# The last pair's exchange through DRAM, and a score product moved in turn 1, in a fused macaron block

## The chip, the cores and the metric

The kernel runs on one core of a Trainium2 chip. The metric is the device time of one execution in microseconds. The profile's time axis starts at the span's start; the span is a little shorter than the device time.

## The reference

The reference is one transformer block of the macaron kind on x of shape 8 x 512 x 128 (batch, tokens, width), all in float32:

```python
x = x + 0.5 * ffn(layernorm(x))
x = x + attn(layernorm(x))
x = x + 0.5 * ffn(layernorm(x))

# attn: 16 heads of rank 64
xq = einsum('btd,hrd->bthr', x, Q); xk = einsum('bud,hrd->buhr', x, K)
a  = softmax(einsum('bthr,buhr->bthu', xq, xk) / sqrt(128), axis=u)
out = einsum('bthu,bud,hde->bte', a, x, VO)

# ffn: three blocks; each: linear, layernorm, gelu, linear, plus its input
# linear: dequantized 128 x 128 weight + bias + low-rank term (rank 32)
```

## The kernel before

**Pairs and turns.** The 16 heads of a batch entry are taken two at a time: a `Pair`, 8 pairs for each of 8 batch entries, 64 in all. Two pairs make a turn, so there are 32 turns (`s` = 0 to 31). Turn 1 handles pairs 2 and 3, turn 31 handles pairs 62 and 63. A turn computes its own pairs' scores and softmax and, at the same time, the sums (softmax times values) of the pairs of the turn before.

**One pair.** For each of four chunks `c` of 128 queries: `scores` makes two products (one for each head) into a PSUM tile `ps`, of which there are two; `maxima` (VectorE) takes the negated row maxima `nm`; `exps` (ScalarE) makes `e` and the row sums; `inverse` and `divide` scale the rows (GpSimd takes one head, ScalarE mostly the other); `turn` (VectorE) transposes `e` in blocks of 32 x 32 into `tr`. What is left of the transposition is an exchange of blocks between the four groups of 32 partitions, done by DMA: `exchange` issues 16 DMAs of 128 KB on SyncE's queue, piece n going from partition group i to group j, from `tr` to `eT`. `attend` then multiplies the values `v` with `eT` into the accumulators `acc`.

**Order.** Everything is laid out with `at(t, function)`. The due times `t` (32 units to a turn) only sort the calls; the instructions are issued in that order, and at the end of the kernel every engine's instructions are chained in it, SyncE's and ScalarE's DMA issues included. So an instruction that waits holds up all that comes after it on its engine. `T_SCORES` and its neighbours in `TIMES` hold the due times of the eight chunks x of a turn (x = 0 to 3 the first pair's, 4 to 7 the second's). In a turn, `a.attend(0, k, 2)`, the first sums, are due at 1.9 + 0.43 k. The second score product (x = 1) is due at 1.05 or 2.0.

**When the exchanges are issued.** The first pair's exchange is due at 16.4, the second's at 27.2; `near` says how many of its 16 pieces go out there. The rest (two, where `near` is `NEAR` = 14) goes out in the next turn at 7.5, between the `send` (7.0) and the `fetch` (8.0) of the feed-forward blocks' own exchange. That exchange (`Exchange`) goes through DRAM: `send` writes `zout` to a DRAM tile `far` with one DMA, `fetch` reads it back into `zin` with four, each of which gathers for one partition group.

**The last pair.** Pair 63 keeps its transposed chunks in two halves of the queries, `trs[0]` (chunks 0 and 1) and `trs[1]` (chunks 2 and 3), 1 MB each. `exchange_halves`, due at 22.9 of turn 31, sends 16 pieces of 64 KB for each half: the first half on SyncE's queue, the second on ScalarE's. `attend_half` multiplies them into the tiles `sum0` and `sum1`, eight products for each half; the second half's products come later on TensorE, between those of the last feed-forward blocks and the last layer norms.

Of the kernel before, what the change touches and what calls it, by code (L numbers as in the profile page):

```python
# [10 lines left out]
F32 = mybir.dt.float32  # L11
# [7 lines left out]
def kernel(  # L19
# [26 lines left out]
    nc = tc.nc  # L46
    B, T, D = x.shape
    H, R, _ = wq.shape
# [5 lines left out]
    P = 128  # L54
    NC = T // P
    Q4 = P // 32
# [9 lines left out]
    dram = ctx.enter_context(  # L66
        tc.tile_pool(name="dram", bufs=2, space=bass.MemoryType.DRAM)
    )
# [18 lines left out]
    def bank(name, tag):  # L87
        if tag == "scores":
            p = psum.tile([P, 2, NC, P], F32, tag=tag, name=name, bufs=2)
            return p[:, 0]  # L90
        return psum.tile([P, NC, P], F32, tag=tag, name=name, bufs=1)
# [51 lines left out]
    def load_projections(g0, g1):  # L143
# [24 lines left out]
        out=bias_bc,  # L168
        in_=biases.rearrange("(k two) d -> two k d", two=2)[0].partition_broadcast(P),
# [8 lines left out]
    def at(t, fn, *args):  # L178
        tasks.append((t, len(tasks), fn, args))
# [298 lines left out]
    NEAR, IDLE = 14, (3.75, 8.9)  # L478
# [5 lines left out]
    class Block:  # L484
# [42 lines left out]
        def second(self):  # L527
            self.po = bank(f"po{self.name}", self.tag)
            nc.tensor.matmul(  # L529
                self.po, lhsT=wT[:, 2 * self.k + 1, :], rhs=self.aT, start=True, stop=True  # L530
            )
# [39 lines left out]
    class Part:  # L571
# [14 lines left out]
        p = property(lambda self: self.banks[self.c][1])  # L586
# [113 lines left out]
    TURNS = B * HP // 2  # L700
# [95 lines left out]
    class Pair:  # L796
# [157 lines left out]

        def exchange_halves(self):

            self.eTs = []
            for h in range(2):
                self.eTs.append(self.half(("eT", "tr")[h], f"eT{h}_").rearrange(
                    "p (i a q) -> p i a q", i=Q4, a=2 * NC  # L960
                ))
                for n in range(Q4 * Q4):
                    i = n % Q4
                    j = (i + n // Q4) % Q4
                    queue = nc.scalar if h else nc.sync
                    queue.dma_start(  # L966
                        out=self.eTs[h][32 * j : 32 * (j + 1), i, :, :].rearrange(
                            "p a q -> p (a q)"
                        ),
                        in_=self.trs[h][32 * i : 32 * (i + 1), j, :, :, :].rearrange(  # L970
                            "p a c r -> p (a c r)"
                        ),
                    )

        def attend_half(self, h, p, j, k):

            nc.tensor.matmul(  # L977
                p, lhsT=self.v[:, k, j, :], rhs=self.eTs[h][:, :, j * NC + k, :],
                start=j == 0 and k == 0, stop=j == 1 and k == NC - 1,
            )  # L980
# [46 lines left out]
    def attn_add(b, a):  # L1027
        oT = work.tile([P, NC, P], F32, tag="oT", name=f"oT{b}", bufs=1)
        nc.vector.tensor_tensor(
            oT.rearrange("p c (i q) -> p i c q", q=32), by_chunks(accs[b][0]), by_chunks(a[0]),  # L1030
            ALU.add,
        )

        def turn():
            po.append(transposed(oT, f"pot{b}", "acc1"))

        def add():
            nc.vector.tensor_tensor(xs[b], xs[b], po[0], ALU.add)

        po = []  # L1040
        return turn, add
# [17 lines left out]
    def lay_turn(s):  # L1059

        t = s * SUP
        two = pairs[2 * s : 2 * s + 2]
        last = s == TURNS - 1
        for x in range(2 * NC):
            m, c = two[x // NC], x % NC

            early = last and x > NC + 1
            T_SCORES, T_MAX, T_EXP, T_INV, T_POOL, T_ACT, T_TURN = TIMES[s > 0]

            at(t + (T_SCORES[x] if x != 1 or not s or s % 4 == 2 else 2.0), m.scores, c)  # L1070
            at(t + (T_MAX[x] if x != NC or not last else 12.59), m.maxima, c)
            at(t + (T_EXP[x] if not early else 17.9 + 1.4 * (c - 2)), m.exps, c)
            at(t + (T_INV[x] if not early else 20.1 + 0.1 * (c - 2)), m.inverse, c)
            at(t + (T_POOL[x] if not early else 20.2 + 1.2 * (c - 2)), m.divide, c, 0, "pool")

            late = s and x > 2 * NC - 3 and not last
            kind = s % 4 if s < TURNS - 6 else 4
            ta = T_ACT[x] if not late else (20.7, (23.7, 23.7, 20.72, 21.1, 23.7)[kind])[x % 2]
            engine = "act" if s or x != 2 * NC - 1 else "pool"
            if late and x % 2 and kind == 3:  # L1080
                engine = "vector"
            at(t + (ta if not early else 20.3 + 0.05 * (c - 2)), m.divide, c, 1, engine)
            u = 21.5 + 1.3 * (c - 2) if early else T_TURN[x] if not late else (21.0, (26.5, 26.5, 22.0, 21.2, 27.15)[kind])[x % 2]
            if last and x in (2, 3):
                u = 11.4 + 1.15 * (x - 2)
            at(t + u, m.turn, c)
        at(t + (12.58 if last else 16.4 if s else 13.8), two[0].exchange)
        if last:
            at(t + 22.9, two[1].exchange_halves)
        else:  # L1090
            near = NEAR if s % 4 != 1 and s else Q4 * Q4
            at(t + (27.2 if s else 24.5), two[1].exchange, 0, near)
            if near < Q4 * Q4:
                at(t + SUP + 7.5, two[1].exchange, near)
        if not last:
            a, b = pairs[2 * s + 2], pairs[2 * s + 3]
            for m, u, d in ((a, 21.9, 23.6), (b, 27.0, 28.7)) if s else ():
                at(t + u, m.project_both)
                at(t + d, m.keep_both)
            if not s:  # L1100
                a.lay_project(0, "acc0", 12.6, 15.15)
                a.lay_project(1, "acc1", 15.0, 15.42)
                at(t + 15.06, b.project_both)
                at(t + 18.0, b.keep_both)
        if s:
            at(t + (23.6 if not last else 19.6), two[0].values)
            at(t + (25.3 if not last else 20.4), two[0].keep_values)
        u, d = (20.2, 22.0) if last else (29.7, 31.4)
        if s:
            at(t + u, two[1].values)  # L1110
            at(t + d, two[1].keep_values)
        else:
            two[1].lay_half_values(0, "acc0", 15.05, 18.1)
            two[1].lay_half_values(1, "acc1", 15.75, 18.2)


        if s:
            a, b = pairs[2 * s - 2], pairs[2 * s - 1]
            for m, j, u in ((a, 0, 1.9), (a, 1, 7.1), (b, 0, 12.2)):
                for k in range(NC):  # L1120
                    at(t + u + 0.43 * k, m.attend, j, k, 2)
            for k in range(2) if last else ():

                at(t + T_SCORES[2 * NC - 2] - 0.02 + 0.005 * k, b.attend, 1, k, 2)
            for k in range(2 if last else 0, NC):
                u = 31.8 if k == NC - 1 and s % 4 == 1 and s > 1 and not last else 18.5 + 0.43 * k
                at(t + u, b.attend, 1, k, 1)
        if s and s % (HP // 2) == 0:
            r = s // (HP // 2) - 1
            done, a = [], []  # L1130
            at(t + 17.85, attn_copy, r, a)
            at(t + 20.7, lambda: done.extend(attn_add(r, a)))
            at(t + 22.5, lambda: done[0]())
            at(t + 22.55, lambda: done[1]())
# [59 lines left out]
    t = {k: T0 + v for k, v in START.items() if isinstance(v, float)}  # L1194
# [40 lines left out]
    for m in lay_parts(0, 0, 1, T0, START, banks, (  # L1235
# [6 lines left out]
        c = m.c  # L1242
# [34 lines left out]
    for s in range(TURNS):  # L1277
        lay_turn(s)


    m = Unit(0, 1)
# [6 lines left out]
    for b in range(B):  # L1288
# [3 lines left out]
        if b > 1:  # L1292
            s = (b - 1) * Q - 2
            t = s * SUP
            m = Unit(0, b, s)
# [5 lines left out]
        if b < B - 1:  # L1301
            s = (b + 1) * Q + 1
            t = s * SUP
            m = Unit(1, b, s)
# [9 lines left out]
    t = TURNS * SUP  # L1314
    a, b = pairs[-2:]
# [62 lines left out]
    for m in lay_parts(1, B - 1, 0, E, END, end_banks, (  # L1378
# [5 lines left out]
        c = m.c  # L1384
        for k in range(NB + 1):
            at(E + END["bias"][c], m.bias, k)
        y = work.tile([P, D], F32, tag="ph", name=f"end{c}", bufs=8)
        queue = nc.scalar if c % 2 else nc.sync
# [3 lines left out]
            out=out[B - 1].rearrange("(p c) d -> p c d", c=NC)[:, c, :], in_=y  # L1392
# [55 lines left out]
```

## Time and profile before

| | us |
|---|---|
| device time, median of 3 runs | 1038.91 (1037.84 to 1040.05) |
| profiled execution: device time | 1039.99 |
| profiled execution: span | 1038.2 |
| TensorE matmul busy in the span | 1023.9 (99%) |
| VectorE busy | 852.6 (82%) |
| ScalarE busy | 783.0 (75%) |
| GpSimd busy | 659.2 (63%) |

TensorE's granted clock is full in all 40 slices of the span. A line of the profile names the line of the kernel (L892 the score products, L1012 the sums, L977 the last pair's sums, L991 the exchanges, L966 the last pair's exchange, L443 and L448 the send and the fetch), the engine (PE TensorE, PEld its weight loads, DVE VectorE, ACT ScalarE, POOL GpSimd, SP SyncE; a q behind the name is the engine's queue, as it issues DMAs), the operation, and out<-in by the program's names. In the timeline the first two numbers are start and duration in us, x is a count, and square brackets hold the idle time before the group and what ended it. In the chain of waits the pieces follow each other back from the last instruction, each one released by the one before.

### The profile page before, as it was taken

What the parts mean: (1) busy time and instruction counts of PE and PEld (TensorE: products, weight loads), DVE (VectorE), ACT (ScalarE), POOL (GpSimd) and SP (SyncE); (2) the same over time, 40 slices, a digit from 0 to 9 for tenths busy, and PEclk for the clock granted to TensorE, in tenths of its full rate; (3) what the DMA queues carried; (4) which work ended last, traced back from release to release, by engine and by line L of the source; (5) the groups of instructions that cost most, each with busy time, mean ns of one, the idle gap of its engine ahead of it and who ended that gap; (6) DMA issues with size and microseconds to landing.
All of it is one profiled execution on the core that took longest, in us unless ns stands there. A gap on an engine that the chain in (4) does not pass through costs nothing.

```text
span 1038.2 us, 15565 instructions
## 1 busy us (share of the span) xinstructions
PE 1023.9 (99%) x4358; PEld 544.2 (52%) x4358; DVE 852.6 (82%) x1606; ACT 783.0 (75%) x1689; POOL 659.2 (63%) x622
## 2 busy tenths in 40 slices
PE   9899999999999999999999999999999999999998
PEld 7465554545555545555544555544555554455556
DVE  6878878888888988888898888888888888877755
ACT  4877778777777877787877877887778887777743
POOL 4667556678567775777567784767857565465523
PEclk9999999999999999999999999999999999999999
DMA  6077765778767886878767887678787777677770
GB/s 194 4 180 184 181 145 142 173 191 203 188 157 183 199 193 168 211 172 205 187 155 189 200 214 173 162 191 205 186 200 179 174 183 172 155 177 180 183 162 21
DMA packets 80892, 179.61 MB, mean 173 GB/s; under 512 B 21212, under 2 KB 41256, under 8 KB 80808
## 3 DMA queue, kind: packets, MB, share of 16 engines
q1 hardware_dynamic: 78440, 177.18, 71.5%
q10 hardware_dynamic: 2368, 1.45, 0.6%
q8 instruction: 36, 0.59, 0.3%
q14 instruction: 48, 0.39, 0.1%
HBM read 23.62 MB, written 20.71 MB: 43 GB/s over the span
## 4 chain that ended last, share of the span: by engine, by line
PE 92%; SPq 3%; DVE 2%; ACT 2%; DMA 1%; issue 1%; POOL 0%; DVEq 0%; ACTq 0%; POOLq 0%
PE acc L1012 40%; PE ps L892 21%; PE pv L852 10%; PE pqk L829 10%; PE po L529 3%; PE py L494 3%; SPq L991 2%; PE py L621 1%; ACT e L904 1%; SPq L966 1%; DVE tr L934 1%; DVE nm L899 1%; PE sum L977 1%; DMA eT<-tr 1%; PE pp L610 0%
## 5 line engine op out<-in xcount | busy, mean ns | idle before, releaser
L916 POOL TENSOR_SCALAR e<-e,rden 128x512 f32<-128x512 f32 x257 | 398.9, 1563 | 227.6 <-DVE rden L911 227.0
L904 ACT ACTIVATE e<-ps,nm 128x512 f32<-128x512 f32 x512 | 345.2, 685 | 169.9 <-DVE nm L899 165.8
L1012 PE MATMUL acc<-eT,v 64*128 64x512 f32 (+1 forms) x1756 | 465.0, 592 | 1.4 <-DMA eT<-tr 0.9
L899 DVE TENSOR_REDUCE nm<-ps 128x2 f32<-128x1024 f32 x256 | 301.6, 1209 | 60.2 <-PE ps L892 59.6
L1012 PEld LDWEIGHTS acc<-eT,v 64*128 64x128 f32 (+1 forms) x1756 | 198.5, 187 | 239.0 <-issue 230.5
L934 DVE STREAM_TRANSPOSE tr<-e 128x1024 f32<-128x1024 f32 x252 | 307.6, 1230 | 16.1 <-POOL e L916 5.3
L892 PE MATMUL ps<-qk 64*128 64x512 f32 x1024 | 252.5, 597 | 1.6 <-ACT e L904 0.9
L920 ACT ACTIVATE e<-e,rden 128x512 f32<-128x512 f32 x249 | 170.0, 725 | 0.6 <-DVE rden L911 0.2
L892 PEld LDWEIGHTS ps<-qk 64*128 64x128 f32 x1024 | 98.7, 186 | 118.0 <-issue 83.7
L852 PE MATMUL pv<-vo_sb,axT 128*128 128x256 f32 x512 | 121.7, 380 | 0.9 <-ACT e L904 0.9
L852 PEld LDWEIGHTS pv<-vo_sb,axT 128*128 128x128 f32 x512 | 94.8, 190 | 29.4 <-issue 12.6
L904 ACT ACTIVATION_READ_ACCUMULATOR e<-ps,nm 128x1 f32 x512 | 103.1, 201 | 0.0
L386 POOL TENSOR_TENSOR rstd<-mv,mhalf 128x4 f32<-128x4 f32 x42 | 43.3, 1030 | 81.1 <-DVE mv L380 80.9
L865 ACT COPY v<-pv 128x512 f32<-128x512 f32 x124 | 66.2, 586 | 32.9 <-PE pv L852 32.8
L399 POOL TENSOR_SCALAR z<-y,rstd 128x128 f32<-128x128 f32 x136 | 79.7, 603 | 3.4
L911 DVE RECIPROCAL rden<-den 128x2 f32<-128x2 f32 x256 | 36.7, 143 | 37.9 <-ACT e L904 36.9
L829 PE MATMUL pqk<-axT,qT_w 128*128 128x512 f32 x122 | 62.4, 593 | 0.0
L829 PE MATMUL pqk<-axT,kT_w 128*128 128x512 f32 x122 | 62.3, 592 | 0.0
L835 ACT COPY qk<-pqk 128x1024 f32<-128x1024 f32 x61 | 60.6, 994 | 2.1 <-PE pqk L829 2.1
L494 PEld LDWEIGHTS py<-wC,hT 128*128 128x128 f32 x336 | 43.2, 192 | 18.8 <-issue 15.4
L535 DVE SCALAR_TENSOR_TENSOR hT<-po,cols,hT 128x512 f32<-128x512 f32 x42 | 31.0, 741 | 22.3 <-PE po L529 21.9
L501 DVE TENSOR_TENSOR y<-py,bias_bc 128x512 f32<-128x512 f32 x42 | 28.5, 678 | 22.5 <-PE py L494 22.3
(162 smaller groups left out, 788.8 us busy)
## 6 DMA issues: line engine op xcount, KB each, us to landing
eT<-tr SPq DMA_DIRECT2D x1008, 128.0 KB, 2.3
far<-zout SPq DMA_DIRECT2D x15, 768.0 KB, 3.7
zin<-far SPq DMA_DIRECT2D x60, 192.0 KB, 3.9
far<-zout SPq DMA_DIRECT2D x10, 512.0 KB, 3.1
zin<-far SPq DMA_DIRECT2D x40, 128.0 KB, 2.9
x<-in_L_attn_x_dram SPq DMA_DIRECT2D x7, 256.0 KB, 5.2
out_dram<-x SPq DMA_DIRECT2D x7, 256.0 KB, 4.1
far<-zout SPq DMA_DIRECT2D x6, 256.0 KB, 2.6
```

The lines of the kernel that those rows point to most:

```text
L399: engine.tensor_scalar(z[:, c, :], self.src[:, c, :], self.rstd[:, c : c + 1], None, ALU.mult)
L494: nc.tensor.matmul(self.py[:, c, :], lhsT=hTs[self.b][:, c, :], rhs=wC[:, self.k, :], start=True, stop=True,)
L829: nc.tensor.matmul(self.pg[:, i, :], lhsT=(qT_w, kT_w)[i][:, self.g, :], rhs=xTs[self.b], start=True, stop=True,)
L852: nc.tensor.matmul(p, lhsT=xTs[self.b][:, c, :], rhs=vo_sb[:, 2 * self.g : 2 * self.g + 2, :], start=True, stop=True,)
L865: nc.scalar.copy(self.v[:, c : c + NC // 2], self.pv[:, c : c + NC // 2])
L892: nc.tensor.matmul(ps[:, j, :], lhsT=self.qk[rows, 0, ts(c, P)], rhs=self.qk[rows, 1, :], start=True, stop=True,)
L899: nc.vector.tensor_reduce(self.nm[:, c, :], self.ps[c], AX.X, ALU.max, negate=True)
L904: nc.scalar.activation(e[:, j, :], self.ps[c][:, j, :], AF.Exp, bias=self.nm[:, c, j : j + 1], accum_out=self.den[:, c, j : j + 1],)
L916: (nc.gpsimd if engine == "pool" else nc.vector).tensor_scalar(e, e, r, None, ALU.mult)
L920: nc.scalar.activation(e, e, AF.Copy, scale=r)
L934: nc.vector.transpose(self.tr[:, :, :, c, :], self.e[c].rearrange("p h (k j r) -> p j (h k) r", j=Q4, r=32),)
L1012: nc.tensor.matmul(accs[self.b][i], lhsT=self.v[rows, k, j, :], rhs=self.eT[rows, :, j * NC + k, :], start=first, stop=end and (j == 1 or ...
```

## The change

1. In turn 1 the second score product (x = 1) gets its due time from the table, 1.05, instead of 2.0; it now comes before the first sums in TensorE's order.
2. In turn 30 `near` is 16 instead of 14: the two pieces of pair 61 that went out in turn 31 between `send` and `fetch` go out with the other fourteen.
3. `exchange_halves` sends the first half by one DMA to a DRAM tile and fetches it back by four. Of the second half's 16 pieces, 4 are issued by SyncE between the write and the fetches, 8 by ScalarE, and 4 by SyncE after the fetches.

```diff
         def exchange_halves(self):
-            self.eTs = []
-            for h in range(2):
-                self.eTs.append(self.half(("eT", "tr")[h], f"eT{h}_").rearrange(
+            self.eTs = [
+                self.half(("eT", "tr")[h], f"eT{h}_").rearrange(
                     "p (i a q) -> p i a q", i=Q4, a=2 * NC
-                ))
-                for n in range(Q4 * Q4):
+                ) for h in range(2)
+            ]
+            far = dram.tile([P, Q4, 4 * NC * 32], F32, tag="half", name="far_half", bufs=1)
+            nc.sync.dma_start(out=far, in_=self.trs[0].rearrange("p j a c r -> p j (a c r)"))
+
+            def second(n0, n1, queue):
+                for n in range(n0, n1):
                     i = n % Q4
                     j = (i + n // Q4) % Q4
-                    queue = nc.scalar if h else nc.sync
                     queue.dma_start(
-                        out=self.eTs[h][32 * j : 32 * (j + 1), i, :, :].rearrange(
+                        out=self.eTs[1][32 * j : 32 * (j + 1), i, :, :].rearrange(
                             "p a q -> p (a q)"
                         ),
-                        in_=self.trs[h][32 * i : 32 * (i + 1), j, :, :, :].rearrange(
+                        in_=self.trs[1][32 * i : 32 * (i + 1), j, :, :, :].rearrange(
                             "p a c r -> p (a c r)"
                         ),
                     )
+
+            second(0, 4, nc.sync)
+            for j in range(Q4):
+                nc.sync.dma_start(
+                    out=self.eTs[0][32 * j : 32 * (j + 1)].rearrange("p i a q -> p i (a q)"),
+                    in_=far.rearrange("(i r) j f -> j r i f", r=32)[j],
+                )
+            second(4, 12, nc.scalar)
+            second(12, 16, nc.sync)
...
-            at(t + (T_SCORES[x] if x != 1 or not s or s % 4 == 2 else 2.0), m.scores, c)
+            at(t + (T_SCORES[x] if x != 1 or s < 2 or s % 4 == 2 else 2.0), m.scores, c)
...
-            near = NEAR if s % 4 != 1 and s else Q4 * Q4
+            near = NEAR if s % 4 != 1 and 0 < s < TURNS - 2 else Q4 * Q4
```

## The prediction

> **What bounds the kernel now.** I read the page first (its chain that ended last and its list of DMA issues), then the chain in order of time at the two places that the change touches (turn 1, turn 31), then the timeline there, the waits, and the DMA answer for short windows.
>
> From the page: the chain's shares by engine, and five rows of DMA issues (KB each, median us from issue to landing).
>
> ```profile
> PE 92%; SPq 3%; DVE 2%; ACT 2%; DMA 1%; issue 1%; POOL 0%; DVEq 0%; ACTq 0%; POOLq 0%
> ...
> eT<-tr SPq DMA_DIRECT2D x1008, 128.0 KB, 2.3
> far<-zout SPq DMA_DIRECT2D x15, 768.0 KB, 3.7
> zin<-far SPq DMA_DIRECT2D x60, 192.0 KB, 3.9
> far<-zout SPq DMA_DIRECT2D x10, 512.0 KB, 3.1
> ...
> far<-zout SPq DMA_DIRECT2D x6, 256.0 KB, 2.6
> ```
>
> TensorE sets the time. The 3% of SPq is some 20 us in two stretches in which TensorE's next product needs the last of 16 issues on SyncE: pair 0's exchange (turn 1) and the last pair's first half (turn 31). Turn 1, TensorE's timeline:
>
> ```profile
> 59.73 1.13 PE L892 MATMUL ps<-qk 64*128 64x512 f32 x4
> 61.75 1.29 PE L1012 MATMUL acc<-eT,v 64*128 64x512 f32 x3 [0.89 <-DMA eT<-tr]
> 62.68 0.59 PE L892 MATMUL ps<-qk 64*128 64x512 f32 x1
> ```
>
> The first score product is done, the sums stand next and wait for pair 0's transfers; the second score product is queued behind the first of the sums. Turn 31, the chain:
>
> ```profile
> 985.29 0.27 issue
> 985.56 5.65 PE acc L1012 x24
> ...
> 1007.56 2.03 DMA eT<-tr
> 1009.59 0.14 issue
> 1009.73 2.40 PE sum L977 x10
> ```
>
> and the timeline (queues and TensorE):
>
> ```profile
> 997.81 10.35 SPq L966 DMA_DIRECT2D eT<-tr  x16
> ...
> 1001.44 8.99 ACTq L966 DMA_DIRECT2D eT<-tr  x14
> ...
> 1006.37 1.88 PE L1012 MATMUL acc<-eT,v 128*128 128x512 f32 x4
> ...
> 1009.73 0.45 PE L977 MATMUL sum<-eT,v 128*128 128x256 f32 x1 [1.48 <-DMA eT<-tr]
> ```
>
> SyncE needs 0.64 us for each issue, 16 of them 10.35 us, and the last one's 64 KB lands 2.03 us after its issue began. TensorE runs out of work at 1008.25 and waits 1.48 us. The second half (ScalarE's queue) lands at about 1012; its first product comes at 1014.03, so it sets nothing.
>
> **Part 1: second score product of turn 1 before the sums.** Its due time goes from 2.0 to 1.05, past the sum due at 1.9. It needs a free score bank (the far projection weights leave theirs when ScalarE's copy ends at 58.89) and qk, so it can run from 60.6 to 61.5, inside the gap. It is 4 passes of 0.215 us = 0.86 us. The sums still start at 61.75 (the last transfer but one lands at 61.66) and their second row half at 62.35 (last one: 59.98 + 2.31 = 62.29), so all that follows on TensorE comes 0.86 us sooner. Can the rest keep up? VectorE takes the second maximum straight after the first (62.83 for 64.36); ScalarE's exponentials of the first two products end at 64.4 and 65.8, and the banks of products 3 and 4 are wanted at 65.8 and 66.6; pair 1's last issue starts at 70.16, lands at 72.5, and is wanted at 73.77 - 0.86 = 72.91. Nothing new is late: 0.86 us, and everything after hangs on TensorE's chain, so it is kept. Bounds: 0 (something in turn 1 takes it back) to 0.9.
>
> **Part 2: turn 30 sends all 16 pieces of pair 61 together.** Two pieces came in turn 31, behind the exchange's send, issued at 980.31. The DMA answer for 980.8 to 981.5 has them:
>
> ```profile
> eT<-tr SPq DMA_DIRECT2D x2, 128.0 KB, 4.7
> ```
>
> 4.7 us instead of 2.3: they land at about 985.0 and 985.7, and TensorE, ready at 985.29, starts at 985.56 and has 24 passes done at 991.22, not at 985.29 + 24 x 0.2145 = 990.44: 0.78 us lost. Moved ahead of the send they land near 982.6. The send and the fetch behind it go back by the two issues, 1.2 us; the fetch ended at 984.82, the next exchange starts at 987.28 (it waits 2.4 us for VectorE), and ScalarE reads zin only at 1000.19, so SyncE's slack covers it; without that slack it would be 1.2 us. Of the 0.78 us, 0.70 passes to the seventh maximum, exponential and value product (994.93 -> 994.23), but pair 62's products, now starting at 999.37, cannot start before its last transfer (996.73 + 2.3 + 0.1 = 999.13). So 0.25 us reaches TensorE's end of work before the last pair: 1008.25 -> 1008.0.
>
> **Part 3: first half through DRAM.** 16 issues of 64 KB become one write of 1 MB and four fetches of 256 KB, with four pieces of the second half between. Step by step:
> - The write needs the first half's transposes (997.5, or 996.8 with part 2) and SyncE (pair 62's issues end at 997.32): issue at 997.4. The three send rows rise by 0.55 us for each 256 KB, so 1 MB lands after 4.25 us: 1001.7.
> - The four pieces wait for the last transpose (1000.14, or 999.4): 4 x 0.64 us on SyncE, until 1002.0, or 1002.7 without part 2's shift. The fetches are queued behind that wait; the write's landing is hidden under it.
> - Four fetch issues took 1.73 to 2.66 us elsewhere: the last starts at about 1003.6. The 192 KB row takes 3.9 us; 256 KB adds 0.14: I take 4.1, landing at 1007.7. In the records each transfer holds one of eight semaphores and waits for the one eight before it, which can put the last fetch behind a piece on ScalarE's queue: +0.4 us, so 1008.1.
>
> Is the transfer itself that quick? The 512 KB send at 99.57, seen from 101 to 108, moved at the first rates below (slices of 0.175 us); the half exchanges on both queues together at the second (last column of the windows view):
>
> ```profile
> GB/s 468 445 398 468 398 351 0 0 0 0 0 0 0 0 29 158 240 281 205 181 334 258 293 299 158 258 234 164 0 0 0 0 0 0 0 0 0 0 0 0
> ...
> 1001.60:1007.50 5.90, 5.90 (x21) 3.17 (x20) 1.65 (x3) 0.36 (x1) 0.00 (x0) 1.00 0.86 203
> ```
>
> A send runs at about 400 GB/s, twice the direct exchange. [...]
>
> TensorE starts the last pair at about 1008.15 instead of 1009.73: 1.58 us, part 2's 0.25 included. The bounds: landing at 1006.8 if the fetch takes 3.2 us (the 128 KB fetches took 2.9), then TensorE's 1008.0 is the limit and the gain 1.73; or, with no shift from part 2, the last issue at 1004.6 and 4.7 us (the longest landing of any far or zin transfer), 1009.3: gain 0.3. What follows moves with TensorE: z, wanted at 1013.7, is ready at 1010.31; the accumulators' sum is ready at 1009.05 for 1011.96.
>
> **Part 4: second half on two queues.** ScalarE's queue issues 8 pieces instead of 16, SyncE 4 before the fetches and 4 after. The last four start at about 1004.2 to 1006.8 and land by 1009 (1011 if they wait for the fetches); wanted at 1014.03 - 1.6 = 1012.4. Cost and gain nothing; the cover is 1.4 us. ScalarE is idle 12.4 us there, so its shorter queue frees no one. [...]
>
> **Sum.** 0.86 + 1.58 = 2.44 us. The profiled execution took 1039.99 us (span 1038.2 and 1.8 around it) and would take 1037.5; it lies 1.1 above the median of the three runs, so the median 1038.91 becomes 1036.5.
>
> **Rivals.**
> - *The fetch is late, or one part is taken back.* The last fetch lands at 1008.7 to 1010, as behind a held semaphore or in contention with ScalarE's pieces; or turn 1's gain is eaten by a later turn. For it: 192 KB fetches at 3.9 us are slow beside 2.9 for 128 KB. Against: TensorE's 92%. Gain 0.9 to 1.9: 1037.0 to 1038.0.
> - *Slower: the detour is bound by bytes.* The half crosses the 16 engines twice. If both legs run at the 203 GB/s of the direct pieces and interleave with them, 2.1 MB + 12 x 64 KB = 2.9 MB take 14.2 us from 999.0: landing at 1013.2, TensorE at 1013.3, +3.6, less 0.86: 1041.6. It decides from a landing at 1010.5 on. Against it: the send's 400 GB/s; for it, the fetch's 158 to 334 GB/s in the same row.
> - *The change does nothing measurable.* Part 1's second product finds its bank or the weight load late and the half lands as before at 1009.6: 1038.9.
>
> **How the numbers follow.** Forecast 0.55 (1036.5; own range 1035.4 to 1037.1, since the three runs differ by 1.1 each way about their median); late fetch or one part lost 0.25 (1037.5); bound by bytes 0.12 (1041.6); nothing 0.08 (1038.9). 0.2% is 2.1 us, about what a measurement of this kernel can tell from no change: faster means below 1036.8. Of the forecast's 0.55 about four fifths lie below that, and of the late case a fifth, with part of a luckier run: 0.52 faster, 0.33 same, 0.15 slower. The range runs from 1035.2 (full 2.6 and a run at the low end) to 1039.4, which leaves the byte-bound case out.
>
> **What would show it.** Right: in turn 1 eight score passes before the sums and no wait of 0.89; pair 61's sums starting without a gap; the first `sum` product within 0.3 us of the last `acc` product; the write landing after 4.2 us and the fetches after 4. Wrong: TensorE waiting over 1 us for the fetch, SyncE's fetches starting after 1004, or a new wait of TensorE in turns 2 to 4 that gives the 0.86 us back.

## The result, and the profile after

| | us |
|---|---|
| before, median of 14 runs | 1038.74 (1037.02 to 1041.22) |
| changed kernel, median of 14 runs | 1041.09 (1038.66 to 1045.11) |
| ratio, 95% interval | 1.0024, 1.0013 to 1.0035 |
| changed kernel, profiled execution | 1042.77, span 1041.0 |

The change makes the kernel slower, by 0.13 to 0.35%. The forecast was 1036.5.

Turn 1 went as forecast. TensorE's timeline of the changed kernel (start, duration, engine, line, operation, count; the sums' line is now L1024; a pass is one matmul instruction, and x counts them):

```profile
59.83 1.99 PE L892 MATMUL ps<-qk 64*128 64x512 f32 x8
61.84 3.86 PE L1024 MATMUL acc<-eT,v 64*128 64x512 f32 x15
```

Eight score passes stand in one row and the wait of 0.89 before the sums is gone.

Turn 31 did not. TensorE's timeline there (L1024 the sums of pair 62, L989 those of the last pair):

```profile
984.37 5.32 PE L1024 MATMUL acc<-eT,v 64*128 64x512 f32 x24
...
999.21 2.81 PE L1024 MATMUL acc<-eT,v 128*128 128x512 f32 x6 [1.22 <-issue]
...
1006.18 1.88 PE L1024 MATMUL acc<-eT,v 128*128 128x512 f32 x4
1010.85 4.01 PE L989 MATMUL sum<-eT,v 128*128 128x256 f32 x10 [2.78 <-DMA eT<-tr]
```

Three things are to be seen: a wait of 1.22 us before pair 62's products that before did not have (kernels without the new exchange have it too, as the last experiment takes up); 2.78 us instead of 1.48 before the last pair's sums; and ten passes that take 4.01 us, where the same ten took 2.40. (The bracket names a piece of the second half, which landed at about the same time. The products read only what the four fetches wrote; the last fetch's last semaphore event is at 1010.61.)

The chain of waits of the changed kernel shows the same end:

```profile
1007.30 3.50 DMA eT<-tr
1010.81 0.04 issue
1010.85 4.01 PE sum L989 x10
```

SyncE's queue in the timeline (L963 the write to DRAM, L969 pieces of the second half, L980 the fetches):

```profile
986.52 10.02 SPq L1003 DMA_DIRECT2D eT<-tr  x16
996.65 0.53 SPq L963 DMA_DIRECT2D far_half<-tr  x1
999.09 3.19 SPq L969 DMA_DIRECT2D eT<-tr  x4
1002.40 2.21 SPq L980 DMA_DIRECT2D eT<-far_half  x4
1004.66 3.94 SPq L969 DMA_DIRECT2D eT<-tr  x4
```

The DMA answers for 996 to 999 and for 1002.3 to 1004.65 (KB each, median us from issue to landing, over those transfers whose landing the view can tell, here two of the four fetches), and the windows view (busy time of PE, PEld, DVE, ACT, POOL; then the granted clock, the DMA share and GB/s):

```profile
far_half<-tr SPq DMA_DIRECT2D x1, 1024.0 KB, 4.7
...
eT<-far_half SPq DMA_DIRECT2D x4, 256.0 KB, 5.3
```

```profile
1003.00:1010.70 7.70, 5.06 (x18) 2.41 (x16) 3.81 (x12) 0.00 (x0) 1.03 (x1) 1.00 0.87 211
1010.70:1014.20 3.50, 3.35 (x8) 2.76 (x9) 0.00 (x0) 0.00 (x0) 0.00 (x0) 0.51 0.00 0
1014.20:1018.00 3.80, 3.80 (x22) 3.01 (x21) 0.69 (x1) 0.93 (x3) 0.00 (x0) 1.00 0.02 4
```

While the fetches are under way the DMA engines are 87% busy and move 211 GB/s. Just as the sums start, the granted clock is 0.51: that is why ten passes take 4.01 us. The page's 40 slices don't show it, since 3.4 us at half speed take 7% off a slice of 26 us and the digit stays 9. The trace's clock record has the half clock from 1010.72 for 3.413 us.

One table serves all kernels below. It is made from the starts of TensorE's products in the profiled executions: from the first score product of turn 1 to that of turn 2; from the first score product of turn 31 to the last pass of pair 62's sums; from there to the last pair's first product; from that to the start of the last instruction. The start-up varies between 28.6 and 30.9 us from one execution to the next, and turns 2 to 30 between 881.2 and 883.5, with no relation to the edits that one execution of each can show, so these pieces tell more than single times.

| kernel | turn 1 | turn 31 to last of pair 62 | wait with it | last pair to end |
|---|---|---|---|---|
| before | 31.39 | 34.66 | 2.07 | 28.42 |
| changed | 30.52 | 35.23 | 3.37 | 30.07 |
| parts 1 and 2, old exchange | 30.52 | 35.57 | 1.20 | 28.38 |
| new exchange alone | 31.37 | 35.12 | 4.17 | 31.27 |
| changed, TensorE filled | 30.52 | 35.69 | 3.33 | 28.45 |
| two queues, alternating | 30.54 | 43.21 | 0.43 | 28.18 |
| fetch alone | 30.52 | 35.59 | 1.24 | 28.47 |
| shared queues, no DRAM | 30.51 | 35.64 | 0.43 | 28.20 |
| part 1 alone | 30.52 | 35.53 | 1.16 | 28.43 |
| part 2 alone | 31.37 | 35.24 | 1.22 | 28.33 |
| 32 whole rows a fetch | 30.51 | 35.67 | 0.95 | 28.45 |
| 128 rows a fetch | 30.52 | 35.49 | 0.43 | 28.38 |
| shared, starting later | 30.53 | 35.46 | 0.43 | 28.19 |

0.43 in the fourth column means no wait: two passes of pair 62 lie between. From before to changed: -0.87 in turn 1, +0.57 and +1.30 up to the last pair, +1.65 behind it, and +0.10 of start-up: +2.75, of the 2.78 between the two profiled executions.

### The profile page after: what moved, and what is told of

It reads as the page before. It is cut to its first block, busy times and chain, and to the rows that moved or that the text cites. A ratio compares the mean times of both kernels' runs of the same rounds, so it can differ in the third digit from the quotient of the medians.

```text
span 1041.0 us, 15560 instructions
## 1 busy us (share of the span) xinstructions
PE 1025.9 (99%) x4358; PEld 550.1 (53%) x4358; DVE 852.6 (82%) x1606; ACT 783.3 (75%) x1689; POOL 660.1 (63%) x622
## 4 chain that ended last, share of the span: by engine, by line
PE 92%; DVE 3%; ACT 2%; DMA 1%; SPq 1%; issue 1%; ACTq 0%; POOL 0%; DVEq 0%; POOLq 0%
PE acc L1024 40%; PE ps L892 20%; PE pv L852 10%; PE pqk L829 10%; PE py L494 3%; PE po L529 3%; PE py L621 2%; DMA eT<-tr 1%; ACT e L904 1%; DVE tr L934 1%; SPq L1003 1%; PE sum L989 1%; DVE nm L899 1%; PE pp L610 0%; PE py L198 0%
## 5 line engine op out<-in xcount | busy, mean ns | idle before, releaser
L1024 PE MATMUL acc<-eT,v 64*128 64x512 f32 (+1 forms) x1756 | 464.9, 592 | 1.2 <-issue 1.2
L1024 PEld LDWEIGHTS acc<-eT,v 64*128 64x128 f32 (+1 forms) x1756 | 201.3, 187 | 235.7 <-issue 229.6
L501 DVE TENSOR_TENSOR y<-py,bias_bc 128x512 f32<-128x512 f32 x42 | 28.5, 678 | 22.5 <-PE py L494 22.3
```

The costliest lines, as they stand in the source:

```text
L1024: nc.tensor.matmul(accs[self.b][i], lhsT=self.v[rows, k, j, :], rhs=self.eT[rows, :, j * NC + k, :], start=first, stop=end and (j == 1 or ...
```

## The experiments

### Parts 1 and 2 with the old exchange

The changed kernel with the old `exchange_halves`.

```diff
-    (the new exchange_halves)
+    (exchange_halves as before: 16 pieces on SyncE, 16 on ScalarE)
```

> The changed kernel with the old exchange of the last pair: the product of turn 1 and the two pieces of turn 30 alone. Theory (the loss is all in the detour through DRAM): the chain reaches the last pair's exchange about 0.8 us sooner, 16 direct issues from 996.7 end with a landing near 1008.4, the last pair's sums start near 1008.5 (1009.73 before), at full clock; about 1037.5 us, 1.2 below before. Rival (the moved pieces of turn 30 or the moved product cost something later): no gain or a loss, 1038.7 or more, and the last pair's sums not before 1009.7.

Measured: 1037.12 (1036.49 to 1038.72, 11 runs) against 1038.52; ratio 0.9986, 0.9978 to 0.9995. TensorE's timeline of this kernel (L977 the last pair's sums):

```profile
1004.35 1.88 PE L1012 MATMUL acc<-eT,v 128*128 128x512 f32 x4
1006.85 2.40 PE L977 MATMUL sum<-eT,v 128*128 128x256 f32 x10 [0.61 <-DMA eT<-tr]
```

The ten passes take 2.40 again. So the loss lies in the new exchange, and the other two parts keep a gain.

### The new exchange alone

Before with only the new `exchange_halves`.

```diff
-    (exchange_halves as before)
+    (the new exchange_halves)
```

> The kernel before with the new exchange of the last pair alone (detour through DRAM, second half on two queues). Theory: the last fetch lands over 6 us after its issue, near 1011.4, TensorE waits over 3 us, its granted clock falls to a half for some 3.4 us and the first ten passes of the last pair's sums take 4.0 us instead of 2.4; about 1042, 3.3 above before. Rival (the detour is harmless, the other two parts brought the loss): about 1038, sums starting by 1009.

Measured: 1043.43 (1040.80 to 1045.20, 6 runs); ratio 1.0042, 1.0027 to 1.0057. Its timeline and windows view:

```profile
1011.59 4.61 PE L989 MATMUL sum<-eT,v 128*128 128x256 f32 x10 [3.58 <-DMA eT<-tr]
```

```profile
1010.50:1017.30 6.80, 5.71 (x16) 4.65 (x17) 0.21 (x1) 0.00 (x0) 0.00 (x0) 0.50 0.07 17
```

A longer wait, 3.58 us, and half the clock for 6.8 us. The exchange alone costs more than the whole change, and it costs twice: in the wait, and behind it.

### TensorE kept busy through the wait

20 transposes of the identity into a PSUM bank that the second half overwrites later, ahead of the last pair's sums; all else as in the changed kernel.

```diff
+    def fill(n):
+        for _ in range(n):
+            nc.tensor.transpose(end_sums[1][:, 0:P], ident, ident)
+
+    at(t + 19.9, fill, 20)
     for i in range(2 * NC):
```

> The changed kernel with 20 transposes of the identity on TensorE (some 2.1 us, into a tile not yet in use) ahead of the last pair's sums, where it waits. Theory (the wait of 2.8 us is what makes the clock fall): the wait is filled, the clock stays at full speed, the first ten passes take 2.4 us instead of 4.0 and the kernel takes 1.6 us less than the changed one: about 1039.5. Rival (the clock falls for another reason, or falls later anyway): no difference from the changed kernel, 1041.

Measured: 1040.15 (1038.96 to 1042.85, 11 runs); ratio 1.0015, 1.0005 to 1.0024. TensorE's timeline:

```profile
1004.05 1.88 PE L1024 MATMUL acc<-eT,v 128*128 128x512 f32 x4
1005.77 2.35 PE L1338 MATMUL sum<-ident 128*128 128x128 f32 x20
1008.67 2.40 PE L989 MATMUL sum<-eT,v 128*128 128x256 f32 x10 [0.55 <-DMA eT<-tr]
```

The sums start no sooner (3.33 in the table, 3.37 without the filling), but the ten passes are back at 2.40 and what follows takes 28.45 instead of 30.07. So 1.6 us of the profiled execution's loss is the clock, which doesn't fall when the wait is filled: its mean is 0.999 or 1.000 in all 11 runs. In the medians it is less, 0.9 us, and the two intervals overlap: of the 14 runs of the changed kernel 9 have a mean granted clock of 0.998, like the profiled one (median 1041.14), and 5 have 1.0 (median 1040.3).

### The direct exchange on two queues, alternating

Parts 1 and 2, and each half's pieces sent in turn by SyncE and ScalarE.

```diff
-    queue = nc.scalar if h else nc.sync
+    queue = nc.scalar if n % 2 else nc.sync
```

> The changed kernel, but both halves of the last pair go directly, without DRAM, each half's 16 pieces alternating between SyncE's and ScalarE's queues. Theory (issue time on one queue was the limit before): 8 issues on each queue from about 997.5, the first half lands near 1005, TensorE goes from its last sums into the last pair's without a wait; about 1036.2. Rival (the 16 DMA engines are the limit, a second queue adds nothing): the first half lands as with one queue, near 1008.4, and the time is that of the kernel with the two small parts alone, 1037.5.

Measured: 1043.76 (1043.15 to 1045.59, 5 runs); ratio 1.0048, 1.0035 to 1.0062: a miss. TensorE's and SyncE's timelines:

```profile
1002.53 5.36 PE L1012 MATMUL acc<-eT,v 128*128 128x512 f32 x6 [6.65 <-DMA eT<-tr]
...
1013.77 2.32 PE L977 MATMUL sum<-eT,v 128*128 128x256 f32 x10
```

```profile
984.98 15.01 SPq L991 DMA_DIRECT2D eT<-tr  x15
1000.16 10.39 SPq L966 DMA_DIRECT2D eT<-tr  x16
```

The last pair's half is in time, but pair 62's exchange (L991) is not: its last two issues come at 998.19 and 999.48 instead of 993 to 994. In the traces of before and of the changed kernel the transfers of both queues share eight semaphores in rotation, and an issue whose semaphore is still held comes when the transfer that holds it has landed (in the changed kernel SyncE's fourth piece of the second half at 1001.78, that landing at 1001.76). ScalarE's first pieces stand ahead of pair 62's last two in that rotation, though pair 62's have the earlier due time. They are issued from 996.14 on and had taken the semaphores that SyncE's last two needed: those two start at 998.19 and 999.48, and the pieces that held theirs landed at 998.17 and 999.46. TensorE waits 6.65 us, and its next six passes take 5.36 us where they took 2.81; the granted clock is 0.74 on average from 1003 to 1012.

### The fetch alone

The changed kernel without the second half's transfers; the second half's products read the first half's tile instead.

```diff
-            second(0, 4, nc.sync)
...
-            second(4, 12, nc.scalar)
-            second(12, 16, nc.sync)
...
-                p, lhsT=self.v[:, k, j, :], rhs=self.eTs[h][:, :, j * NC + k, :],
+                p, lhsT=self.v[:, k, j, :], rhs=self.eTs[0][:, :, j * NC + k, :],
```

> The changed kernel without the transfers of the last pair's second half: its products read the first half's tile again, so the second half's sums are left out. Theory (the fetch was late because the second half's pieces shared the 16 engines with it): the four fetches land about 0.7 us apart instead of 1.4, the last one under 5 us after its issue instead of 6.6, near 1008.5; TensorE waits under 0.7 us and its clock stays full. Rival (the fetch from DRAM is that slow by itself): they land 1.4 us apart, the last 6 us or more after its issue, and TensorE waits 2.5 us or more.

Measured, one execution: 1039.06 (before beside it 1038.53). From the semaphore events, the four fetches:

| | issued | landed | from issue |
|---|---|---|---|
| changed | 1002.40, 1003.21, 1003.56, 1004.05 | 1006.43, 1007.84, 1009.23, 1010.61 | 4.03, 4.63, 5.66, 6.55 |
| fetch alone | 1001.46, 1001.82, 1002.30, 1002.76 | 1004.92, 1006.20, 1007.42, 1008.63 | 3.46, 4.37, 5.13, 5.86 |

With nothing else on the DMA engines the last fetch still takes 5.86 us, and they land 1.24 us apart: 256 KB at about 212 GB/s. The landing is 1.98 us sooner than in the changed kernel; 1.29 of that is the earlier issue (0.31 of it because this execution starts turn 31 sooner), only 0.69 the company of other transfers. Neither expectation is met in full: the gaps and the last landing are nearer to the rival's, but TensorE waits only 0.65 us. The fetch is slow by itself, and not the whole of the delay.

### What is slow in the fetch: rows and partitions

Both as in the fetch alone, and in both the blocks land in other places than the exchange needs. One reads 32 whole rows of 8 KB into their 32 partitions, so its packets are larger (from 999 to 1005, the write's end included, 54 of 182 are under 8 KB, in the fetch alone 312 of 377) but its destination is the same 32 partitions; the other reads one 2 KB block of every row into all 128 partitions, so its packets are small (251 of 348 under 8 KB).

```diff
-    out=self.eTs[0][32 * j : 32 * (j + 1)].rearrange("p i a q -> p i (a q)"),
-    in_=far.rearrange("(i r) j f -> j r i f", r=32)[j],
+    out=self.eTs[0][rows].rearrange("p i a q -> p (i a q)"),       # 32 rows
+    in_=far.rearrange("p j f -> p (j f)")[rows],
```

```diff
+    out=self.eTs[0][:, j, :, :].rearrange("p a q -> p (a q)"),     # 128 rows
+    in_=far[:, j, :],
```

> As the run with the fetch alone (second half's transfers left out), but each of the four fetches reads 32 whole rows of 8 KB back into its 32 partitions, so that blocks are not exchanged. Theory (a fetch into only 32 partitions is slow, whatever it reads): the fetches still land 1.2 us apart, the last 5.5 to 6 us after its issue. Rival (gathering 2 KB pieces at 8 KB distance from DRAM is slow): 0.7 us apart, the last under 4.8 us after its issue.

> As the run with the fetch alone (second half's transfers left out), but each of the four fetches reads one 2 KB piece of every row into all 128 partitions, so that blocks are not exchanged; the pieces in DRAM are 2 KB at 8 KB distance as in the real fetch. Theory (32 partitions are slow): the fetches land 0.7 us apart, the last under 4.8 us after its issue. Rival (the 2 KB pieces are slow): 1.2 us apart, the last 5.5 us or more after its issue.

The DMA answers, 32 whole rows first, 128 rows second (three of the four landings told):

```profile
eT<-far_half SPq DMA_DIRECT2D x4, 256.0 KB, 4.9
```

```profile
eT<-far_half SPq DMA_DIRECT2D x4, 256.0 KB, 3.8
```

Whole rows change little: landings 1004.10, 1005.32, 1006.48, 1007.60, still 1.17 us apart on average. All 128 partitions do: 1005.45, 1006.13, 1007.00, 1007.62, 0.72 us apart, the last 3.98 us after its issue, and TensorE doesn't wait. The 128-row form reads the same bytes of DRAM as the fetch alone, fetch by fetch; only their destination differs. So in these three runs neither the size of the reads nor DRAM sets the price of the fetch, but that each transfer goes into only 32 partitions (1.24 and 1.17 us apart, against 0.72 into 128). The detour as it is cut here, one fetch for each destination group, has to do that. An exchange that sorts the blocks on the way into DRAM, so that each fetch could land in all 128 partitions, was not run; whether the detour has a cheaper form is open.

### Part 1 alone

```diff
-  at(t + (T_SCORES[x] if x != 1 or not s or s % 4 == 2 else 2.0), m.scores, c)
+  at(t + (T_SCORES[x] if x != 1 or s < 2 or s % 4 == 2 else 2.0), m.scores, c)
```

> The kernel before with the turn-1 product alone. Theory: from turn 1's first score product to turn 2's the time falls by 0.87 us (31.39 to 30.52) and nothing after it changes, with pair 62's last transfer landing 2.4 us after its issue and the wait before the last pair's sums at 1.5 us as before; about 1037.8. Rival (the shift is taken back at pair 62's transfers, as it seemed in the changed kernel): the distance from turn 31's first score product to the last sums of pair 62 grows by 0.5 us or more over 34.66.

Measured: 1037.55 (1036.52 to 1039.81, 12 runs) against 1038.53; ratio 0.9990, 0.9980 to 0.9999. Turn 1 takes 30.52, and from turn 31 to the last pair's sums it takes 36.69 (before 36.73), so nothing is given back there. The rival's sign did come, 35.53 up to pair 62's last sums where before took 34.66, since pair 62's last transfer took 3.23 us; but the wait behind it is shorter by as much (1.16 for 2.07). Its sums of pair 61:

```profile
983.86 5.32 PE L1012 MATMUL acc<-eT,v 64*128 64x512 f32 x24
```

24 passes in 5.32 without a wait, though here the two late pieces are where they were before and take 4.1 and 3.9 us.

### Part 2 alone

```diff
-            near = NEAR if s % 4 != 1 and s else Q4 * Q4
+            near = NEAR if s % 4 != 1 and 0 < s < TURNS - 2 else Q4 * Q4
```

> The kernel before with the two moved pieces of turn 30 alone. Theory (the sooner start of the last pair's exchange runs into pair 62's last transfers): pair 61's sums start without their 0.3 us wait, but pair 62's last transfer lands about 3 us after its issue instead of 2.4, its first product waits, and the last pair's sums start where they did (36.7 us after turn 31's first score product): no difference, 1038.6. Rival (the 0.25 us that I forecast are kept): the last pair's sums start 0.2 us sooner, 36.5.

Measured: 1038.42 (1037.40 to 1041.69, 12 runs); ratio 0.9998, 0.9988 to 1.0007. By the times part 2 can't be told from nothing, and 0.25 us can't be excluded either: the interval runs from 1.2 us faster to 0.7 slower. The one profiled execution shows what the rival named: the last pair's sums start 36.46 us after turn 31's first score product, 0.27 sooner than before, although pair 62's last transfer took 2.97 us and its products waited 1.24, as the theory had it. With part 1 beside it the gain isn't there: 36.77 with both parts, 36.69 with part 1 alone.

### Part 1 and a direct exchange that shares the queues

SyncE's pieces of the first half come first, and ScalarE starts with a piece of the second half, which has to wait for the last transpose (and for pair 62's last transfer, whose source is the buffer it writes into); so ScalarE comes in late enough to hold no semaphore that pair 62 needs.

```diff
+            pieces(0, 0, 10, nc.sync)      # (half, from, to, queue)
+            pieces(1, 0, 1, nc.scalar)
+            pieces(0, 10, 16, nc.scalar)
+            pieces(1, 1, 8, nc.sync)
+            pieces(1, 8, 16, nc.scalar)
```

> The turn-1 product alone with a direct exchange of the last pair: 10 pieces of the first half on SyncE, then one piece of the second half and the first half's other 6 on ScalarE (so that ScalarE's first issue comes after pair 62's exchange has left SyncE), then the second half's rest on both. Theory (issue time on one queue was the limit, and the exchange on two queues failed only because ScalarE's early pieces took semaphores for which pair 62's last pieces then waited): the first half lands about 3.5 us sooner than on one queue, TensorE goes into the last pair's sums without a wait; 0.87 + 1.48 = 2.3 us below before, 1036.2. Rival (ScalarE's pieces hold SyncE's up again, or the engines are full): the wait before the last pair's sums stays at 1 us or more; 1037.6 or more.

Measured: 1036.60 (1035.37 to 1038.72, 9 runs) against 1038.53; ratio 0.9977, 0.9968 to 0.9986. It beats before and the changed kernel; its interval overlaps with that of part 1 alone. TensorE's timeline:

```profile
1006.95 1.88 PE L1019 MATMUL acc<-eT,v 128*128 128x512 f32 x4
1008.67 2.32 PE L984 MATMUL sum<-eT,v 128*128 128x256 f32 x10
```

No wait, full clock. Each of the pieces on the two queues that run side by side lands 1.9 to 2.3 us after its issue; the last of the first half is in at 1006.04, 2.6 us before it is wanted. What the detour was for is had without it.

### The same, starting later

The first piece on each queue is one of the second half, so that no transfer follows straight behind pair 62's. This asks why pair 62's last transfer takes 2.95 us in the changed kernel and 2.36 in before, and makes its products wait.

```diff
+            pieces(1, 0, 1, nc.sync)
+            pieces(1, 1, 2, nc.scalar)
+            pieces(0, 0, 8, nc.sync)
+            pieces(0, 8, 16, nc.scalar)
+            pieces(1, 2, 9, nc.sync)
+            pieces(1, 9, 16, nc.scalar)
```

> As the shared direct exchange with the turn-1 product, but the first piece on each queue is one of the second half's, so that all of it waits for the last transpose and starts some 2.5 us later; then 8 pieces of the first half on each queue, then the rest. Theory (the last pair's first transfers, right behind pair 62's, make pair 62's last one land 0.6 us late, for which its products wait): it lands 2.4 us after its issue, pair 62's products start 0.6 us sooner, the first half still lands before TensorE wants it; about 1036.0, 0.6 below the run with the first half ahead. Rival (its late landing has another reason): it still lands 3 us after its issue and the time is 1036.6 or more.

Measured: 1036.26 (1035.43 to 1038.09, 12 runs) against 1038.06; ratio 0.9984, 0.9975 to 0.9992, the same as the kernel above within the intervals. The next transfers now start 2.5 us later, at 997.67, when pair 62's last one has landed (997.48), and still that one takes 3.00 us and its products wait 1.46. So it isn't slowed by what follows it. All the profiled executions but that of before show 2.75 to 3.23 us there; the profile of before was the exception, and why is open.

## Why the prediction was wrong

The prediction's times in turn 31 stand on the axis of before without part 1. The changed kernel starts turn 31 about 0.75 us sooner, so each is read 0.75 earlier here.

**Part 1** was right: 0.86 forecast, 0.85 to 0.88 measured in every kernel that has it, and the run of part 1 alone is faster by 0.1 to 2.1 us.

**Part 2** was right in what it moves; what it is worth stays open. The 0.78 us were read from one execution, in which the two late pieces took 4.9 and 4.7 us. In the execution of part 1 alone the same two pieces were no trouble, with the new exchange alone they cost 0.27 us (24 passes in 5.59), and in that with the shared queues they took 2.5 us. The 0.25 shows in the execution of part 2 alone and not beside part 1.

**Part 3, the write,** held: issue at 996.65 where 996.65 was forecast, landing after 4.73 where the slope of the send rows gave 4.25.

**Part 3, the issues.** The last fetch was issued at 1004.05 instead of 1002.85. The four pieces began 0.44 late (999.09, where 998.65 was forecast with part 2's shift and 999.39 without): the last transpose was done at 998.62, but they write into the buffer that pair 62's exchange reads, and its last transfer landed at 998.91, a wait that the prediction didn't have. From there it took 3.31 us until the first fetch's issue instead of 2.56: the fourth was issued at 1001.78, when the piece on ScalarE's queue that held its semaphore had landed (1001.76). The second fetch waited in the same way (1003.21 after 1003.20), but from the first fetch's issue to the last one's it was 1.65 us, where 1.6 was forecast. The prediction named this kind of wait and allowed 0.4 for it; it looked for it at the fetches, not at the pieces ahead of them.

**Part 3, the fetch: the step that failed.** "The 192 KB row takes 3.9 us; 256 KB adds 0.14: I take 4.1." The 0.14 is the slope of the send, one DMA that reads all 128 partitions. The fetch rows themselves, 2.9 us at 128 KB and 3.9 at 192 KB, rise by 1.0 for 64 KB, which gives 4.9 at 256 KB; the fetch alone measured 4.75 as the median of the four and 5.86 for the last. The second slip lies in that: a row's median is that of four transfers that queue behind each other, and what TensorE needs is the last. With the other transfers it was 6.55 instead of 4.1, so 2.45 us late on top of an issue 1.2 us late.

**The clock: a step that was missing.** No case priced what a wait does to TensorE beyond its length. A wait of 1.48 us had cost nothing in before; 2.78 us cost another 1.65 behind it. In the changed kernel's clock record the half clock lasts 3.413 us; the full stretch before it is 1000.105 us, 293 times 3.41333, and the one behind it 27.307, eight times that. In before the full stretch is 1027.412, 301 times that. In the exchange alone the half clock lasts about twice as long, 6.8 us. Fixed windows of 3.41 us are the author's estimate from these records. By them the window that ended at 1010.72 held 0.75 us of matmuls and 2.66 of idling, and in the exchange alone the one before the fall, at about 1010.5, held about 0.9 and 2.5; both were idle for about three quarters. That the place of the windows against the wait decides which of the 14 runs fall would fit the 9 and 5, but was only argued.

The errors add up. The profiled execution was to take 1039.99 - 2.44 = 1037.55 and took 1042.77, 5.22 more: sums 3.45 late (1010.85 for 1007.40), 1.65 of clock, 0.10 of start-up.

**Part 4** was right that the second half sets nothing: with the clock full, the kernels that share its transfers take 28.2 to 28.5 from the sums to the end, like before. Its pieces weren't free, though: their semaphores held up the fetches (the second was issued at 1003.21, after a landing at 1003.20).

**The rivals.** "Bound by bytes" was given 0.12 and named 1041.6; the measurement is 1041.09. Its rate was near, 203 GB/s against 211. Its landing was not: it has 1012.4 on this axis for 1010.61, because the write ran faster (4.73 us from issue to landing, where 1 MB at 203 GB/s takes 5.2), and its 3.6 us are in fact about 1.9 of wait and 1.65 of clock. The nearness of its time to the measured one is thus partly luck. And it had the legs compete with the direct pieces, while the fetch alone showed that the fetch needs no competitor to be slow.

## What to carry to other kernels

Price a transfer by rows of its own shape, above all by how many partitions it lands in (here 256 KB landed every 1.24 us in 32 partitions and every 0.72 in 128), and take the last of a group in flight, not the median (5.86 us against 4.75 in the fetch alone). Price a wait of TensorE that grows past what the profile of before shows by the clock as well (here 1.48 us was free of it and 2.78 was not, in 9 of 14 runs), and look at the granted clock in windows of a few us behind it, since the page's slices can hide it (here 3.41 us at half speed in a slice of 26). When issue time on one queue is the limit (here 16 issues took 10.35 us and TensorE waited 1.48), share the same pieces between two queues before making them larger (the wait was gone), and let the second queue start late enough that its transfers hold no semaphore that the first one's older issues still need (with the alternating queues TensorE waited 6.65 us).

## What was not expected of the hardware

- Without the second half's pieces, the fetches of 256 KB into 32 partitions landed 1.24 us apart on average where 2 KB blocks were read and 1.17 where whole rows were (212 and 225 GB/s); into 128 partitions 0.72 (362 GB/s).
- In the profiled executions a TensorE wait of 2.78 us halved the clock for 3.41 us, one of 3.58 for about 6.8; one of 1.48 didn't.
- A single execution's stall of 0.78 us (pair 61) came again only once and in part (0.27 us, with the new exchange alone), and its lack of one (pair 62) in no other. A gain read from one stall of one profile needs a second profile.
